# Fetching more of a graph layer's edge tiles by rows, and a later fall of GpSimd's lead

## The chip, the cores and the metric

The kernel runs on one core of one Trainium2 chip. A core has five engines that run their own instruction streams and wait for each other through semaphores: TensorE (PE in the profile, its weight loads PEld), VectorE (DVE), ScalarE (ACT), GpSimd (POOL) and SyncE (SP). Transfers are started by instructions on SP, ACT or POOL and are carried out by the core's 16 DMA engines. The metric is the device time of one execution in microseconds (us), lower is better.

## The reference, cut to what matters

A relational graph layer with 12500 nodes, 256 features, 8 relations and 212500 edges; the edges are sorted by their destination, and each node has an edge to itself.

```python
h = relu(layernorm(x))                       # 12500 x 256
hx = einsum('ni,rio->rno', h, weight)        # 8 relations
msg = hx[edge_type, src]                     # one row for each edge
agg = segment_sum(msg, dst, 12500)
out = x + agg * sqrt(0.5) + bias + (h @ loop_weight) * sqrt(0.5)
```

## The kernel before, in words

The sum over the edges is taken before the product with the weights: for each relation and destination node the rows of h of the edges' sources are added up, and the result is multiplied by the weight of that relation.

**Tiles.** The edges are cut into tiles of 128, two tiles to a unit. For a tile the 128 source rows of h (1 KB each) are brought from the chip's memory into a buffer `msg`, one row to a partition. VectorE makes a one-hot matrix `oh` of the edges' destinations and relations (L1066). TensorE multiplies the two (`edge_sums`, L1105: four matmuls in the profile for a tile, 6296 in all, so 1574 tiles), VectorE adds a unit's sums into a ring `acc` of node columns (L1141). When a group of 128 nodes is complete, 18 products with `w` and `wl` (L1321, two matmuls each in the profile) are spread between the next tiles' sums, VectorE adds the result to x (L1307, L1338), and SyncE stores it.

**How a tile's rows arrive.** There are two ways. Most tiles are gathered by GpSimd with one indirect DMA (L1009, `gather`). Some tiles are fetched by rows (`single_rows`, `begin_fetch`, `load_sources`): SyncE and ScalarE load the 128 source offsets into registers (L1030, five loads: two on SP for 28 and 32 rows, three on ACT for 24, 20 and 24 rows) and issue a DMA of 1 KB for every row (L1038), 60 on SP and 68 on ACT. GpSimd does nothing for such a tile. Before, the tiles with t % 54 of 25 or 53 are fetched in this way from tile 161 on, and besides them the last tile and the fifteenth from the end: 54 tiles. The first tiles, gathered from x and normalised by ScalarE in place, are all GpSimd's.

**The order of the work** is written out by hand: one loop over the tiles `t` emits the instructions of all engines, and each engine executes its own in that order. At tile t the loop emits the gathers up to `goal(t)`: the lead of GpSimd over the sums is 64 tiles at first, falls to 24 (`NEXT`), and near the end by one for every `SLOPE` = 5 tiles down to 8 (`CLOSE`). A gather also waits for the last finished unit of sums at that place, so the lead is a limit at run time too. A fetch by rows is begun 40 tiles ahead of its use (`FAR`), its instructions stand from 8 tiles later (`HOLD`) at up to four on each of the two engines for each tile. The buffers are a pool of 33 pairs, given out in the order of the loop; the first row or gather into a buffer waits for the sums that read it last. TensorE waits for all 128 rows of a fetched tile through a counter (L1101).

After the first 190 us or so ScalarE has hardly anything but the rows to do: its queue holds them and five small loads (`spans`, L441) that a later block of edges needs on VectorE. SyncE's queue also has the loads of x and h for the groups (`xr`, `hr`, L1258), the edges' indices (L432) and the stores of the results (L1350).

Of the kernel before, what the change touches and what calls it, by code (L numbers as in the profile page):

```python
# [40 lines left out]
NEAR = 8  # L41
# [17 lines left out]
SLOPE = 5  # L59
NEXT = 24  # L60
CLOSE = 8

SINGLE = 54
PLACED = (25, 53)
CLOSING = 15
SOONER = 64
FETCH = 4
SOURCES = ((0, 28, "SP"), (28, 24, "ACT"), (52, 20, "ACT"), (72, 32, "SP"), (104, 24, "ACT"))
# [193 lines left out]
def kernel(  # L262
# [22 lines left out]
    NT = plan.NT  # L285
# [57 lines left out]
    with ExitStack() as main:  # L343
# [623 lines left out]

        def in_turn(t):

            return t % SINGLE in PLACED  # L970

        def filled(t):

# [2 lines left out]

        def single_rows(t):

            return ((t in (NT - 1, NT - CLOSING) or in_turn(t) and t + 2 * NEAR < NT)
                    and state["h32"] is not None and t // QUAD * QUAD >= state["h32"] + LATE + AHEAD)  # L980

        def begin_fetch(t):
# [10 lines left out]
        def gather(t):  # L993
            if t % PAIR == 0 and t not in msg:
                room(t)
            if t % QUAD:
                kind[t] = kind[t - 1]
            else:
                kind[t] = "h" if state["h32"] is not None and t >= state["h32"] + LATE else "x"
            table = {"h": h32, "x": x}[kind[t]]  # L1000
            b, i, u = place_of(t)
            if single_rows(t) and t not in fetched and t - done["tile"] >= FAR:
                begin_fetch(t)
            if t in fetched:
                return
            at = i * P + u
            n = filled(t)
            of = direct[:, i : i + 1] if t < PAIR else gidx[b][:, at : at + 1]
            i = nc.gpsimd.indirect_dma_start(  # L1009
                out=msg[t][:n], out_offset=None, in_=table[:, :],  # L1010
                in_offset=bass.IndirectOffsetOnAxis(ap=of[:n], axis=0))
            if kind[t] == "h":
                n = landed[t] = len(landed)
                i.then_inc(landings[n % LANDINGS], 16)
                tc.no_tile_sem_insts.add(i.ins.name)
                tc.add_to_no_dep_group(f"landed{t}", i.ins)
            if "unit" in latest:
                tc.add_manual_dep(
                    i.ins, latest["unit"], SYNC_DEP, reason="no faster than the sums")

        def goal(t):

            lead = max(NEXT, AHEAD - max(0, t - NARROW) // SLOPE)
            lead = min(lead, max(CLOSE, (NT - t) // SLOPE))
            return min(t + lead + 1, STARTED + STEEP * (t // PAIR * PAIR))

        def load_sources(t, r0, count, engine):
# [364 lines left out]
        with tc.manual_schedule():  # L1392
# [150 lines left out]
            for t in range(NT):  # L1543
                done["tile"] = t
                if t + FAR >= gathered and single_rows(t + FAR):
                    begin_fetch(t + FAR)
                while gathered < min(NT, goal(t)):
                    gather(gathered)
                    gathered += 1
# [125 lines left out]
```

## Time and profile before

| What | Value |
| --- | --- |
| Time of the kernel before, median of 3 runs | 1936.13 us (1932.9 to 1936.15) |
| The profiled execution's own time | 1932.58 us |
| Its span from the first to the last instruction | 1930.9 us |
| Busy share of the span: PE, DVE, POOL, ACT | 87%, 69%, 75%, 7% |
| Mean granted TensorE clock | 0.96 |
| Gathers of h by GpSimd | 1432 |
| Rows fetched on ACT and on SP | 3672 and 3240 |

A line of a group has the line of the kernel, the engine, the operation, what it writes and reads, the count, then busy time and the mean in ns of one, then the engine's idle time just before and what ended it. In the lists of one source line, "min/median/max" are durations in ns, and the two times behind them are the starts of the first and the last instruction in us from the span's start. Instructions that issue DMAs or load registers on SP and ACT (SPq, ACTq) are not counted as busy: ACT's 7% says nothing of how full its queue is.

### The profile page before, as it was taken

The numbers are of one execution on the slowest core, as the hardware profiler recorded it, in microseconds if no ns is written. First come the engines' busy times: TensorE is split into PE (matmuls) and PEld (weight loads), VectorE is DVE, ScalarE is ACT, GpSimd is POOL, SyncE is SP. The second block draws the span as 40 slices with busy tenths as digits, with TensorE's granted clock in tenths as the row PEclk, the third lists the DMA queues.
The fourth block names the chain that finished last, engine by engine and source line by source line (L and its number), as shares of the span: only waits on it lengthen the run. The fifth ranks groups of instructions, "written<-read, shape, count | busy, mean of one in ns | idle before, by whom it ended". The sixth has DMA issues, their size and how long they took to land.

```text
span 1930.9 us, 41561 instructions
## 1 busy us (share of the span) xinstructions
PE 1684.4 (87%) x10136; PEld 1441.3 (75%) x10136; DVE 1325.9 (69%) x3353; ACT 132.0 (7%) x286; POOL 1445.7 (75%) x1546
## 2 busy tenths in 40 slices
PE   2367999999889999989888989898989888999998
PEld 2356889899778777777777777777777777777887
DVE  7888768976567965658766656776566885665653
ACT  6964000000000000000000000000000000000000
POOL 7777777777777777777777777777777777777774
PEclk9568999999999999999999999999999999999999
DMA  9974455445544444454444454444445444444443
GB/s 322 382 222 146 121 141 142 142 132 141 145 126 140 123 131 138 126 144 130 132 131 121 136 139 131 130 130 132 131 128 142 122 130 132 132 127 132 128 109 88
DMA packets 159057, 278.88 MB, mean 144 GB/s; under 512 B 35819, under 2 KB 110168, under 8 KB 158808
## 3 DMA queue, kind: packets, MB, share of 16 engines
q0 software_dynamic: 72960, 199.33, 36.3%
q1 hardware_dynamic: 77000, 73.08, 12.3%
q10 hardware_dynamic: 8848, 3.78, 1.0%
q8 instruction: 80, 1.31, 0.3%
q14 instruction: 169, 1.38, 0.2%
HBM read 250.45 MB, written 25.60 MB: 143 GB/s over the span
## 4 chain that ended last, share of the span: by engine, by line
PE 31%; POOL 27%; DMA 20%; issue 11%; DVE 7%; ACT 3%; DVEq 0%; SPq 0%; POOLq 0%; ACTq 0%
POOL msg L1009 27%; DMA msg<-h,gidx 19%; PE po L1321 16%; PE ps L1105 15%; ACT msg L931 1%; DVE acc L1141 1%; DVE stats L887 1%; DMA xt<-in_x_dram 1%; DVE oh L1066 1%; DVE moves L478 1%; ACT xt L931 1%; DVE acc L1183 1%; PE pt L1165 1%; ACT acc L1154 0%; DVE fixed L480 0%
## 5 line engine op out<-in xcount | busy, mean ns | idle before, releaser
L1009 POOL DMA_INDIRECT msg<-h,gidx x1432 | 1360.2, 950 | 439.1 <-issue 375.9
L1105 PEld LDWEIGHTS ps<-oh,msg 128*128 128x128 f32 x6296 | 915.7, 196 | 384.7 <-DMA msg<-h,gidx 261.9
L1105 PE MATMUL ps<-oh,msg 128*128 128x136 f32 (+1 forms) x6296 | 998.9, 288 | 197.6 <-DMA msg<-h,gidx 131.5
L1321 PE MATMUL po<-w,acc 128*128 128x256 f32 (+1 forms) x3136 | 881.5, 386 | 4.2 <-DVE acc L1141 3.0
L1141 DVE TENSOR_TENSOR acc<-acc,ps 128x352 f32 x788 | 406.5, 516 | 363.0 <-PE ps L1105 351.3
L1321 PEld LDWEIGHTS po<-w,acc 128*128 128x128 f32 (+1 forms) x3136 | 515.3, 192 | 42.0 <-issue 11.3
L1183 DVE SCALAR_TENSOR_TENSOR acc<-types,pt 128x256 f32<-128x256 bf16 x720 | 258.9, 412 | 76.0 <-PE pt L1165 65.3
L1066 DVE TENSOR_TENSOR oh<-fixed,cols 128x544 f32<-128x544 f32 x394 | 281.4, 714 | 0.0
L1321 PE MATMUL po<-wl,self_t 128*128 128x256 f32 (+1 forms) x392 | 111.8, 409 | 5.4 <-DVE self_t L1170 4.6
L1009 POOL DMA_INDIRECT msg<-in_x_dram,gidx x86 | 81.5, 948 | 26.2 <-issue 23.5
L1321 PEld LDWEIGHTS po<-wl,self_t 128*128 128x128 f32 (+1 forms) x392 | 71.2, 203 | 13.5 <-DVE self_t L1170 5.9
L1307 DVE TENSOR_TENSOR xr<-xr,po 128x256 f32<-128x256 f32 (+1 forms) x98 | 40.5, 413 | 19.1 <-PE po L1321 19.0
L1338 DVE TENSOR_TENSOR xr<-xr,po 128x256 f32<-128x256 f32 (+1 forms) x98 | 41.2, 421 | 10.4 <-PE po L1321 7.0
L478 DVE TENSOR_SCALAR moves<-fixed 128x336 int32<-128x336 int32 (+1 forms) x96 | 44.6, 465 | 5.2 <-DVE acc L1141 3.7
L931 ACT ACTIVATE msg<-msg,shift,rstd 128x256 f32<-128x256 f32 x88 | 44.8, 587 | 6.9 <-DVE stats L895 4.5
L480 DVE COPY_PREDICATED fixed<-moves,fixed 128x335 int32<-128x335 int32 (+7 forms) x96 | 41.6, 433 | 3.3
L1237 DVE CAST types<-pt 128x512 bf16<-128x512 f32 x23 | 15.9, 690 | 40.0 <-PE pt L1233 39.1
L1170 DVE COPY self_t<-pt 128x256 f32<-128x256 f32 (+1 forms) x98 | 40.6, 414 | 2.2 <-PE pt L1165 2.2
L1165 PE MATMUL pt<-ident,hr 128*128 128x128 f32 (+1 forms) x196 | 38.3, 278 | 2.9 <-DMA hr<-h 1.5
L931 ACT ACTIVATE xt<-xt,shift,rstd 128x256 f32<-128x256 f32 x66 | 33.7, 587 | 9.8 <-DVE shift L928 9.8
L1221 DVE TENSOR_TENSOR of<-pt,line 22x512 bf16<-22x512 f32 x23 | 15.7, 682 | 20.4 <-PE pt L1214 20.2
L1165 PEld LDWEIGHTS pt<-ident,hr 128*128 128x128 f32 (+1 forms) x196 | 25.3, 149 | 5.3 <-DMA hr<-h 1.8
(179 smaller groups left out, 373.8 us busy)
## 6 DMA issues: line engine op xcount, KB each, us to landing
msg<-h ACTq DMA_DIRECT2D x3672, 1.0 KB
msg<-h SPq DMA_DIRECT2D x3240, 1.0 KB
msg<-h,gidx POOLq DMA_INDIRECT x1432, 5.1
hr<-h SPq DMA_DIRECT2D x23, 512.0 KB
xr<-in_x_dram SPq DMA_DIRECT2D x23, 512.0 KB
out_dram<-xr SPq DMA_DIRECT2D x22, 512.0 KB
xt<-in_x_dram SPq DMA_DIRECT2D x16, 512.0 KB
h<-xt SPq DMA_DIRECT2D x16, 512.0 KB
```

What stands on the lines that cost most here:

```text
L478: nc.vector.tensor_single_scalar(m, packed[:, :n], 1 << (bit + k), op=ALU.bitwise_and)
L480: nc.vector.copy_predicated(packed[:, : n - (1 << k)], m[:, 1 << k :], packed[:, 1 << k : n])
L931: nc.scalar.activation(row, row, AF.Relu, bias=shift[:n, j : j + 1], scale=rstd[:n, j : j + 1])
L1009: i = nc.gpsimd.indirect_dma_start(out=msg[t][:n], out_offset=None, in_=table[:, :], in_offset=bass.IndirectOffsetOnAxis(ap=of[:n], axis=0))
L1066: j = nc.vector.tensor_tensor(o[:, k : k + v, :i, :width], iota_f[:, :width].unsqueeze(1).unsqueeze(1).to_broadcast([P, v, i, width]), of. ...
L1105: j = nc.tensor.matmul(ps[:, c, first : first + width], m[:used, c * P : (c + 1) * P], o[:used, :width], start=(i == 0 and c == 0), stop=( ...
L1141: i = nc.vector.tensor_tensor(a, a, ps[:, c], op=ALU.add)
L1165: in_run("turns", nc.tensor.transpose(pst[:, c, :n], rows_[:n, c * P : (c + 1) * P], ident[:n, :n]), c == KC - 1)
L1170: nc.vector.tensor_copy(got["self", g][:, :, :n], pst[:, :, :n])
L1183: i = nc.vector.scalar_tensor_tensor(acc[:, :, r, s0 : s0 + n], of, float(r + 1), pst[:, :, :n], op0=ALU.is_equal, op1=ALU.mult)
L1321: i = nc.tensor.matmul(got["out", g][:n], lhs, rhs, start=(r == R and c == 0), stop=(r == R - 1 and c == KC - 1))
L1338: nc.vector.tensor_add(rows_[:n, k, :], rows_[:n, k, :], got["out", g][:n])
```

## The change: what it does

```diff
-SINGLE = 54
-PLACED = (25, 53)
-CLOSING = 15
+SINGLE = 24
+PLACED = 13
+ENDING = 2
...
         def in_turn(t):
 
-            return t % SINGLE in PLACED
+            return t % SINGLE == PLACED
...
         def single_rows(t):
 
-            return ((t in (NT - 1, NT - CLOSING) or in_turn(t) and t + 2 * NEAR < NT)
+            return ((t == NT - 1 or in_turn(t) and t + 2 * NEAR < NT)
                     and state["h32"] is not None and t // QUAD * QUAD >= state["h32"] + LATE + AHEAD)
...
         def goal(t):
 
             lead = max(NEXT, AHEAD - max(0, t - NARROW) // SLOPE)
-            lead = min(lead, max(CLOSE, (NT - t) // SLOPE))
+            lead = min(lead, max(CLOSE, (NT - t) // ENDING))
             return min(t + lead + 1, STARTED + STEEP * (t // PAIR * PAIR))
```

A tile is now fetched by rows when t % 24 is 13, from tile 157 to tile 1549, and the last tile, 1573, which is again 24 tiles on. That is 60 tiles instead of 54, with a distance of 24 instead of 28 and 26 in turn. The fifteenth tile from the end is gathered. The division of a fetched tile between SP (60) and ACT (68) stays. The lead of the gathers falls from 24 when 48 tiles are left (before: 120) and reaches 8 at 16 (before: 40).

On GpSimd six gathers fewer stand in the queue; these are its rows of gathers (`direct` and `x` are the first tiles, `flag` is read at the end):

```order
 L1009 DMA msg<-in_x_dram,direct 128x256 x2
 L1009 DMA msg<-in_x_dram,gidx 128x256 x86
-L1009 DMA msg<-h_57,gidx 128x256 x1432
+L1009 DMA msg<-h_57,gidx 128x256 x1426
 L1638 TENSOR_LOAD flag
 L1648 COMPARE_AND_BRANCH
```

Six gathers left, and nothing else of GpSimd's moved.

On ScalarE this is the place of the first `spans` load among the rows of the first fetched tiles (`single` holds the offsets of the sources):

```order
 L1030 TENSOR_LOAD single
 L1038 DMA msg<-h_57 1x1024 x24
+L1030 TENSOR_LOAD single
+L1038 DMA msg<-h_57 1x1024 x24
+L1030 TENSOR_LOAD single
+L1038 DMA msg<-h_57 1x1024 x20
+L1030 TENSOR_LOAD single
+L1038 DMA msg<-h_57 1x1024
 L441 DMA spans<-in_dst_dram 128x2x1
```

45 rows and three loads of registers more stand ahead of the `spans` load here; between a fetched tile's rows and the next one's there is no other instruction on this engine, before and now.

On SyncE this is the place where the first fetched tile begins; `hr` is a load of four groups' rows of h. Before:

```order
L1258 DMA xr<-in_x_dram 128x4x256
L1258 DMA hr<-h_57 128x4x256 x2
L1030 TENSOR_LOAD single
L1038 DMA msg<-h_57 1x1024 x28
L1030 TENSOR_LOAD single
```

And now:

```order
L1258 DMA xr<-in_x_dram 128x4x256
L1258 DMA hr<-h_57 128x4x256
L1030 TENSOR_LOAD single
L1038 DMA msg<-h_57 1x1024 x11
L1258 DMA hr<-h_57 128x4x256
L1038 DMA msg<-h_57 1x1024 x17
```

One load of `hr` now stands behind the first rows of the first fetched tile. TensorE's and VectorE's instructions stand in the same order as before.

## The prediction

> **What bounds the kernel now.** I read the page's sums and chain first, then GpSimd by stretches and row by row, then the two queues that fetch rows, because the change moves tiles from the one to the others.
>
> ```profile
> span 1930.9 us, 41561 instructions
> PE 1684.4 (87%) x10136; PEld 1441.3 (75%) x10136; DVE 1325.9 (69%) x3353; ACT 132.0 (7%) x286; POOL 1445.7 (75%) x1546
> ...
> PE 31%; POOL 27%; DMA 20%; issue 11%; DVE 7%; ACT 3%; DVEq 0%; SPq 0%; POOLq 0%; ACTq 0%
> ```
>
> PE has the larger busy share, but the chain runs through POOL, its issue gaps and the landing of its gathers for more than half of the span. Gathers by stretches (POOL busy), four of POOL's rows near the end, and its waits after 1780 us:
>
> ```profile
> 200.00:300.00 100.00, 75.78 (x80) 1.00 0.49 135
> 900.00:1000.00 100.00, 75.59 (x81) 0.97 0.47 132
> 1800.00:1900.00 100.00, 75.60 (x81) 0.98 0.42 117
> ```
> ```profile
> 1779.53 0.95 POOL L1009 DMA_INDIRECT msg<-h,gidx  x1 [0.30 <-issue]
> 1780.78 0.95 POOL L1009 DMA_INDIRECT msg<-h,gidx  x1 [0.30 <-issue]
> ...
> 1910.85 0.95 POOL L1009 DMA_INDIRECT msg<-h,gidx  x1 [0.30 <-issue]
> 1912.10 0.95 POOL L1009 DMA_INDIRECT msg<-h,gidx  x1 [0.30 <-issue]
> ```
> ```profile
> POOL msg L1009 <- issue: 25.9, 85, 0.3
> POOL msg L1009 <- PE ps L1105: 6.7, 22, 0.3
> ```
>
> The pace never changes: 107 gathers start between 1779.53 and 1912.10, so one every 132.57/106 = 1.2507 us, and 0.3 us is the longest gap, whatever ended it. GpSimd works without a pause; its "75%" is 0.95 of 1.25 us. It is the bound, with TensorE just behind:
>
> ```profile
> PEld ps L1105 <- DMA msg<-h,gidx: 261.9, 401, 3.0
> ```
>
> TensorE waits for gathers 401 times. It has the room to run faster:
>
> ```profile
> 900.00:1000.00 100.00, 89.46 (x526) 74.38 (x524) 76.10 (x198) 0.00 (x0) 75.59 (x81) 0.97 0.47 132
> ```
>
> **The rows' own queues.** ScalarE's 7% hides its queue. Rows and register loads over the run, and SP's waits:
>
> ```profile
> L1038 ACTq DMA_DIRECT2D msg<-h x3672: 227/228/804, 198.4 to 1865.8; - x194
> L1038 SPq DMA_DIRECT2D msg<-h x3240: 224/228/1812, 198.4 to 1858.9; - x191
> ```
> ```profile
> L1030 ACTq TENSOR_LOAD <-single x162: 1532/1790/2890, 182.4 to 1855.9; - x162
> ```
> ```profile
> SPq L1038 <- PE ps L1105: 304.6, 43, 47.5
> ```
>
> 54 tiles of 68 rows; at present the queues wait for free buffers (SP 43 times), so rows come well before their use. What a fetched tile costs ACT when nothing holds it is read from three places: the rows alone of one tile, the loads of three tiles near the end, and the loads of fourteen tiles early on.
>
> ```profile
> L1038 ACTq DMA_DIRECT2D msg<-h x23: 227/228/233, 666.1 to 673.3; - x23
> ```
> ```profile
> L1038 ACTq DMA_DIRECT2D msg<-h x68: 227/228/470, 1202.0 to 1227.9; - x68
> L1038 SPq DMA_DIRECT2D msg<-h x60: 227/228/304, 1202.0 to 1224.3; - x60
> ```
> ```profile
> L1030 ACTq TENSOR_LOAD <-single x7: 1582/1819/1832, 1780.4 to 1837.9; - x7
> ```
> ```profile
> L1030 ACTq TENSOR_LOAD <-single x43: 1539/1783/1903, 224.5 to 635.1; - x43
> ```
>
> A row takes 7.2/22 = 0.33 us of the queue (0.23 is the DMA, the rest a register move and gaps). One tile: 25.9 us from its first row to its last, two loads among them, 0.2 for the last row, 1.8 for the load ahead and 0.2 of gaps, 28.1 us. Near the end (57.5 us for two tiles) 28.75; with the third, of 28.1, 28.5 on average. Early on 410.6/14 = 29.3 us a tile, row behind row. SP's 60 rows need 22.5 and two loads of about 2.1, one of them inside: 25 us.
>
> **The change, part by part.**
>
> GpSimd: six gathers fewer, 6 x 1.2507 = 7.5 us. If it stays the bound, the last gather ends 7.5 us earlier and 1932.58 becomes 1925.1. TensorE could follow: 24 tiles cost it 24 x 1.2 x 0.89 = 25.7 us of work, by the stretch 900 to 1000 (83 tiles, 89% busy), where GpSimd gives it 24 tiles in 23 x 1.2507 = 28.8.
>
> ScalarE: 28.8 us is also all that it now has for a fetched tile, where it had 26 x 1.2507 = 32.5 on average. Its own need was 28.1 to 29.3. So the question of this change is whether one queue keeps up, and it is settled by a sum over the run: 60 tiles, one after the other, in one stream.
>
> It can't start sooner than the buffer is free. The first row was held until 198.4 us by the sums of the tile 66 before; the first fetched tile is now 157 instead of 161, and tiles go by at one a microsecond there:
>
> ```profile
> 200.00:300.00 100.00, 57.45 (x396) 57.36 (x395) 1.00 0.49 135
> 300.00:400.00 100.00, 57.86 (x400) 57.74 (x398) 1.00 0.50 142
> ```
>
> 396/4 = 99 tiles in 100 us, so it starts 4 us sooner, at 194.4, and its rows are out 26.1 us later (as before, where the second tile's first load is at 224.5), at 220.5. 59 tiles follow, then the last rows land, and behind them come the last tile's sums and the tail. This is the tail, with the last products:
>
> ```profile
> 1914.97 2.56 PE ps L1105 x20
> ...
> 1917.95 7.19 PE po L1321 x32
> ```
>
> The last tile's four matmuls start 0.7 us before 1917.53, at 1916.8, so the tail is 1930.9 - 1916.8 = 14.1 us. For the landing no view gives the rows alone; the gathers on the same chip, with rows running all the time (300 to 500 us) and with pauses (900 to 1100 us), took
>
> ```profile
> DMA to landing us min/median/max: 7.1/11.4/12.2
> ```
> ```profile
> DMA to landing us min/median/max: 3.3/4.6/5.9
> ```
>
> from the issue on. I take 6 us, between 4 and 11. With c us for a tile and the 1.7 us around the span: 1.7 + 220.5 + 59c + 6 + 14.1 = 242.3 + 59c. Before's 1932.58 is reached at c = 28.65, GpSimd's 1925.1 at 28.5.
>
> Which c? Bounds are 28.1 and 29.3. The early row is the state to which the change leads: SP and ACT without a pause, and gathers landing late. From tile 157 TensorE passes 24 tiles in 24 us while ACT needs 29, so the 40 us by which the rows are ahead (tile 157's sums are due 66 tiles after tile 91's, at about 261) are used up after eight tiles, near tile 350. From there on TensorE waits at every fetched tile; SP, which needs less, comes to be held by buffers, which eases the traffic a little. I take 29.3 for the first 15 of the 59 and 28.8 for the other 44, above the 28.5 of the end, because that stretch began after pauses: 439.5 + 1267.2 = 1706.7, so 242.3 + 1706.7 = **1949.0 us**, 16 us over the profiled execution.
>
> TensorE's waits for rows do not add to this: the work of 24 tiles fits into c, and GpSimd's gathers run ahead meanwhile, up to 24 tiles, which is one whole distance.
>
> The lead at the end I cost at nothing: GpSimd never waited more than an issue gap after 1780 us, so a limit that it doesn't reach may be eased for free. If TensorE stands at tile 1549 for its rows, the old rule would have allowed 8 tiles ahead, leaving 16 gathers, 20 us, still inside the 28.8 before the last tile's rows; without that cover it would be worth up to 16 gathers' part beyond it, none here. The gather in place of the fifteenth tile's rows is in the six.
>
> What stands behind the rows: on SP one `hr` load moves behind rows that wait until 194, its users come 30 us and more later; on ACT the `spans` loads of 0.4 us, which VectorE needs some 30 us after their present issue:
>
> ```profile
> 281.82 0.41 ACTq L441 DMA_DIRECT2D spans<-in_dst_dram  x1
> ```
>
> With ACT late that cover shrinks to about ten tiles, 10 us. Nothing; if it is gone, a few us at each of five places, in which TensorE mostly waits anyway.
>
> Two rules of the Trainium skill speak against my sum; both lead to the first rival below. The Trainium skill's page "DMA: Bandwidth & Descriptors", section "Latency and other measured facts", has a floor of about 0.6 us for a register load; by it the three would take 1.8 us, c would be 25 and the answer 1925. The rows above show 1.79 for each one, and they decide. The same page of the Trainium skill, section "Issuing engines are not separate DMA queues", says that all queues share the 16 engines and that several issuers save only issue time, usually small beside the transfer; by it the rows would cost no queue anything and the answer would again be 1925. The later landing fits its first half; its second doesn't fit the 28 us of issue for a tile.
>
> **The rivals.**
>
> *GpSimd stays the bound* (the other side: faster). It needs c up to 28.6 over the whole run. For it: single tiles of 28.1, and the last three. Against it: fourteen in a row of 29.3, without a pause as now. Price: 1925.1 up to c = 28.5, then rising to 1932.
>
> *A tie.* c between 28.64 and 28.78 gives 1932 to 1940; ScalarE takes away what GpSimd gains. For it: the 28.75 of the two tiles from 1780 on.
>
> *The traffic feeds on itself.* Rows never pause, landings stay at 11 us, and c stays at 29.3 to the end: 242.3 + 5 + 59 x 29.3 = 1976. Against it: the transfers for groups and indices are spread over a longer time, and SP will pause.
>
> *The change doesn't do what it says*: the end's lead is such a part; it moves no time in any of the cases.
>
> **How the numbers follow.** Forecast (c from 28.78 to 29.2) 0.56; GpSimd stays the bound 0.18; tie 0.13; traffic 0.13. What can be told from no change is 0.2%, some 4 us around 1936.13, so from 1932.3 to 1940: faster 0.18, same 0.13, slower 0.69. The time is the forecast's, 1949. It is made against 1932.58, and the median shown is 3.6 above that; I don't add this, because what sets the time changes. The forecast's own range is 1940 to 1965. Taking in GpSimd's 1925.1 and most of the traffic's case leaves about 0.15 outside: 1925 to 1970.
>
> **What would show it.** Right: ACT's loads at three per 28.8 us or more from the first to the last, without a wait for buffers after the first tile; its last row near 1925; TensorE's largest waits now for the rows (L1105 or its counter at L1101, on `msg<-h` from ACT) from about 450 us on, and fewer for gathers; GpSimd with pauses longer than 0.3 us behind the sums, and fewer than 80 gathers in 100 us. Wrong: GpSimd still at 1.25 us without a pause, its last gather near 1904.6, and ACT waiting for buffers. Also wrong in size: c well under 28.6 because rows come faster when GpSimd is slowed, or a tail longer than 14 us.

## The result, and the profile after

The change makes the kernel slower: 1965.36 us median of four runs (1961.28 to 1966.87) against 1934.68 us for the kernel before (1932.9 to 1936.15), a ratio of 1.016 with a 95% interval of 1.0146 to 1.0174. The forecast was 1949.0 us. The profiled execution took 1961.28 us, 28.7 us more than the profiled one of before; the forecast had 16.4 us. The median lies 16.4 us above the forecast: 12.3 of them are in the profiled execution, and the other 4.1 are there because the profiled execution was the quickest of the four. The direction and the mechanism were right, the size was not.

The chain of waits of the kernel after, first by engine, then by line:

```profile
ACTq 43%; PE 27%; DMA 10%; issue 10%; DVE 4%; ACT 4%; SPq 2%; PEldq 0%; DVEq 0%
ACTq L1038 35%; PE po L1321 14%; PE ps L1105 12%; DMA msg<-h 9%; ACTq L1030 8%; ACT msg L931 2%; SPq L1038 1%; DVE stats L887 1%; ACT xt L931 1%; DVE acc L1141 1%; ACT acc L1154 0%; DMA nat_s<-in_src_dram 0%; PE pt L1214 0%; DVE oh L1066 0%; ACT unused L900 0%
```

Before, ScalarE's queue had 0% of this chain and POOL 27%. Now ScalarE's row issues (L1038) and register loads (L1030) have 43%, the landing of the rows 9%, and POOL is gone from it. The list of waits says the same from the other side (columns: total us, times, longest):

```profile
PEld ps L1105 <- PEq L1101: 197.7, 47, 9.9
PE ps L1105 <- PEq L1101: 181.2, 47, 9.5
POOL msg L1009 <- PE ps L1105: 82.4, 157, 3.6
```

L1101 is the counter of a fetched tile's rows. TensorE waits there at 47 of the 60 fetched tiles, and its 261.9 us of waits for gathers are no longer in the list. GpSimd, which before stood still for 0.3 us at most once 200 us were over, now waits up to 3.6 us for sums, because its lead is used up. By stretches (the fifth pair of columns is POOL):

```profile
200.00:300.00 100.00, 96.14 (x637) 88.42 (x636) 71.26 (x163) 0.00 (x0) 75.59 (x81) 1.00 0.49 136
400.00:500.00 100.00, 83.16 (x509) 74.47 (x507) 58.08 (x132) 0.00 (x0) 69.53 (x73) 0.91 0.46 125
1200.00:1300.00 100.00, 84.47 (x521) 77.19 (x522) 73.15 (x177) 0.00 (x0) 75.54 (x80) 0.93 0.47 126
```

TensorE is busy 96% until the head start of the rows is spent, and GpSimd loses gathers (73 in place of 80) where its lead first runs into the limit. The rows and the register loads on the queues:

```profile
L1038 ACTq DMA_DIRECT2D msg<-h x4080: 227/228/552, 195.7 to 1942.1; - x195
L1038 SPq DMA_DIRECT2D msg<-h x3600: 224/228/2792, 195.7 to 1887.3; - x190
...
L1030 ACTq TENSOR_LOAD <-single x180: 1446/1787/2987, 183.1 to 1932.7; - x180
```

From the end of each tile's last row on ScalarE (records of L1038, 68 to a tile) the first tile was out at 221.8 us, the sixteenth at 667.4 and the sixtieth at 1942.4. So a fetched tile took (1942.4 - 221.8)/59 = 29.16 us of ScalarE's queue: 445.6/15 = 29.7 in the first fifteen, 1275.0/44 = 28.98 in the others. The last tile's sums:

```profile
1943.59 2.71 PE L1105 MATMUL ps<-oh,msg 128*128 128x104 f32 x20
1946.74 7.17 PE L1321 MATMUL po<-w,acc 128*128 128x256 f32 x32 [0.43 <-DVE acc L1141]
```

The four matmuls of the last tile start some 0.7 us before 1946.3, so 1945.5; the landing was 3.1 us and the tail 1959.6 - 1945.5 = 14.1. The prediction's sum with measured terms is 1.7 + 221.8 + 59 x 29.16 + 3.1 + 14.1 = 1961.1, and the execution took 1961.28.

### The profile page after: what moved, and what is told of

It reads as the page before. It is cut to its first block, busy times and chain, and to the rows that moved or that the text cites. A ratio compares the mean times of both kernels' runs of the same rounds, so it can differ in the third digit from the quotient of the medians.

```text
span 1959.6 us, 43202 instructions
## 1 busy us (share of the span) xinstructions
PE 1662.4 (85%) x10136; PEld 1504.6 (77%) x10136; DVE 1323.5 (68%) x3353; ACT 132.0 (7%) x286; POOL 1440.4 (74%) x1540
## 3 DMA queue, kind: packets, MB, share of 16 engines
q14 instruction: 182, 1.49, 0.3%
## 4 chain that ended last, share of the span: by engine, by line
ACTq 43%; PE 27%; DMA 10%; issue 10%; DVE 4%; ACT 4%; SPq 2%; PEldq 0%; DVEq 0%
ACTq L1038 35%; PE po L1321 14%; PE ps L1105 12%; DMA msg<-h 9%; ACTq L1030 8%; ACT msg L931 2%; SPq L1038 1%; DVE stats L887 1%; ACT xt L931 1%; DVE acc L1141 1%; ACT acc L1154 0%; DMA nat_s<-in_src_dram 0%; PE pt L1214 0%; DVE oh L1066 0%; ACT unused L900 0%
## 5 line engine op out<-in xcount | busy, mean ns | idle before, releaser
L1105 PEld LDWEIGHTS ps<-oh,msg 128*128 128x128 f32 x6296 | 960.9, 202 | 339.3 <-PEq L1101 197.7
L1105 PE MATMUL ps<-oh,msg 128*128 128x136 f32 (+1 forms) x6296 | 976.0, 288 | 244.2 <-PEq L1101 181.2
L1321 PE MATMUL po<-w,acc 128*128 128x256 f32 (+1 forms) x3136 | 914.5, 398 | 6.0 <-DVE acc L1141 4.5
L1321 PEld LDWEIGHTS po<-w,acc 128*128 128x128 f32 (+1 forms) x3136 | 534.4, 199 | 49.1 <-issue 11.7
L1237 DVE CAST types<-pt 128x512 bf16<-128x512 f32 x23 | 15.9, 690 | 37.9 <-PE pt L1233 37.4
L1221 DVE TENSOR_TENSOR of<-pt,line 22x512 bf16<-22x512 f32 x23 | 15.7, 682 | 27.4 <-PE pt L1214 27.3
```

Of the source, the lines that this page charges most:

```text
L1105: j = nc.tensor.matmul(ps[:, c, first : first + width], m[:used, c * P : (c + 1) * P], o[:used, :width], start=(i == 0 and c == 0), stop=( ...
L1321: i = nc.tensor.matmul(got["out", g][:n], lhs, rhs, start=(r == R and c == 0), stop=(r == R - 1 and c == KC - 1))
```

## The experiments

There were eighteen runs. The first fourteen fell on chips on which before itself takes 2389 to 2418 us in place of 1935, so every ratio here is to runs of before on the same chip.

### On the chips of 1935 us

**Rows 72 to 103 by one transfer (less_rows_e).** ScalarE issues what the change issues; SyncE issues 28 single rows and one transfer of 32 rows in place of 60 single ones, and has one register load in place of two. TensorE's counter waits for 97 arrivals in place of 128.

```diff
+            if r0 == 72:
+                def fetch_block(k=fetched[t]):
+                    j = nc.sync.dma_start(msg[t][r0 : r0 + count, :], h32[:count])
...
-                j = nc.tensor.wait_ge(counters[k % COUNTERS], 16 * P * (k // COUNTERS + 1))
+                j = nc.tensor.wait_ge(counters[k % COUNTERS], 16 * (P - 31) * (k // COUNTERS + 1))
```

> The change with rows 72 to 103 of every fetched tile fetched by one transfer of 32 neighbouring rows of h; those are not the rows of the sources, so this part of the result is not the reference's. Where before takes about 1935 us: on ScalarE's records of the change a row takes 337 ns while SyncE issues none and 347 ns while it does, 0.7 us a tile, and sp52_less gained 1.5 us a tile from 27 rows fewer; by that ScalarE's tile falls from 29.16 to 28.2 to 28.6, 1925 to 1930 us, ratio 0.995 to 0.998. If the surplus is ScalarE's own: 1.011 to 1.016. Where before takes about 2400 us: 0.986 again.

Measured: 1927.54 us against 1934.72, ratio 0.9964 (0.995 to 0.9978), as the theory of the traffic has it; 1927.54 is 7.2 us below before, and six gathers are 7.5. Its chain, its waits and ScalarE's rows (line numbers are 13 higher):

```profile
ACTq 38%; PE 27%; issue 11%; POOL 8%; DMA 7%; DVE 5%; ACT 3%; SPq 0%; DVEq 0%; PEldq 0%; POOLq 0%
```
```profile
POOL msg L1009 <- issue: 401.3, 1315, 0.3
...
PEld ps L1118 <- PEq L1114: 115.4, 40, 5.9
PEld ps L1118 <- DMA msg<-h,gidx: 79.7, 131, 2.2
...
POOL msg L1009 <- PE ps L1118: 44.4, 140, 2.0
```
```profile
L1051 ACTq DMA_DIRECT2D msg<-h x4080: 227/228/858, 194.5 to 1902.6; - x195
```

The same 4080 rows are issued 39.5 us sooner. Reckoned as above, a tile takes 28.51 us of ScalarE's queue in place of 29.16. From the records the 68 issues of a tile last 16.58 us together in place of 17.17, and of them 3.8 in place of 7.4 last over 300 ns; the three loads (5.2 and 5.3 us) and the rest, register moves and gaps (6.7 in both), are what they were. No gap on ScalarE is over 1 us in either run behind the first fetched tile, so its queue is not held by buffers. So 0.59 of the 0.65 us is row issues that had been drawn out beside SyncE's single rows. 28.51 is just under GpSimd's 23 x 1.2507 = 28.77: both queues are about equal, waits for gathers are back, and GpSimd keeps its pace.

The traffic shows in the gathers too. The last column is the median time from issue to landing in us; the view has a landing for 21 of the gathers before, for 126 in less_rows_e and for 21 in even64_e. Before:

```profile
msg<-h,gidx POOLq DMA_INDIRECT x1432, 5.1
```

with the transfer of 32 rows:

```profile
msg<-h,gidx POOLq DMA_INDIRECT x1426, 2.8
```

and with 64 single rows on each engine (the next run):

```profile
msg<-h,gidx POOLq DMA_INDIRECT x1426, 9.5
```

The landings of more gathers can be read from the semaphores' updates: a gather's landing is told by sixteen increments, and over a thousand gathers of each run have all sixteen. The fifteenth comes 2.8 us after the issue (median) in all four kernels, the sixteenth after 5.1 us before, 9.3 in the change, 3.2 in less_rows_e and 9.5 in even64_e. So one of the sixteen is late, and the more so the more single rows there are. The single rows themselves stand in line: each is one packet of 1 KB that lasts 0.06 to 0.09 us, but a ScalarE row's packet, taken in the order of issue, ends 2.8 us after its issue before (median), 7.0 in the change, 1.3 in less_rows_e and 9.1 in even64_e. This would fit single rows that all go through one of the 16 DMA engines; the trace doesn't number the engines, so that place is argued, not shown.

The Trainium skill's page "DMA: Bandwidth & Descriptors", section "Issuing engines are not separate DMA queues", says that transfers of all issuers interleave on the same 16 engines; these landings agree. Its remark that the issue is usually small beside the transfer does not hold for rows of 1 KB: here the issue sets the time, and 32 issues on one queue lengthen those of the other.

**64 rows on each engine (even64_e).**

```diff
-SOURCES = ((0, 28, "SP"), (28, 24, "ACT"), (52, 20, "ACT"), (72, 32, "SP"), (104, 24, "ACT"))
+SOURCES = ((0, 32, "SP"), (32, 24, "ACT"), (56, 16, "ACT"), (72, 32, "SP"), (104, 24, "ACT"))
```

> The change split 64 to 64. Where before takes about 1935 us: ScalarE's tile is 27.8 us, under GpSimd's 28.8, so GpSimd is the bound again: 1925 to 1928 us, ratio 0.995 to 0.997; if the loss is not ScalarE's queue, 1.016. Where before takes about 2400 us: 1.073 again.

Measured: 1947.08 us against 1934.72, ratio 1.0062 (1.0048 to 1.0077). The split is worth some 18 us against the change (1.0062 for 1.016), so the rival that it is worth nothing falls; but the kernel is still slower than before, so the expectation falls too. Chain, waits, and the rows:

```profile
SPq 35%; PE 28%; DMA 15%; DVE 9%; issue 9%; ACT 3%; DVEq 0%; PEldq 0%; ACTq 0%
```
```profile
PEld ps L1105 <- PEq L1101: 192.9, 41, 13.4
```
```profile
L1038 SPq DMA_DIRECT2D msg<-h x3840: 227/228/1729, 193.6 to 1919.6; - x192
L1038 ACTq DMA_DIRECT2D msg<-h x3840: 227/228/776, 193.6 to 1880.9; - x192
```

ScalarE is done 61 us sooner than in the change and has 0% of the chain; SyncE has taken its place. From the first tile's end (217.5 us) to the last's (1919.9) a tile took SyncE 28.85 us on average, not 26.4. One tile in this mean took 46.2 us: SyncE stood still ahead of two loads of the edges' indices, which the profile puts down to the landing of earlier loads:

```profile
SPq L432 <- DMA hr<-h: 9.9, 1, 9.9
SPq L436 <- DMA nat_s<-in_src_dram: 6.5, 1, 6.5
```

The 44 tiles ahead of this stop took 28.87 us each without a gap of 1 us, which is already over GpSimd's 28.77; the 14 behind it took 27.56. What the kernel would take without the stop no run shows. The last rows needed 10.7 us to land: 1.7 + 217.5 + 59 x 28.85 + 10.7 + 14.1 = 1946.2, where the profiled execution took 1946.59. I had costed SyncE's tile from 25 us, one tile's rows and two loads. In the change's own trace its first eighteen tiles, with next to no pauses, took 26.3, 26.7 and 27.4 us (means of six), with 0.5 to 1.1 us for the loads of x and h that go through the same queue, and row issues that grew as on ScalarE. The four rows brought their own cost and again longer issues: 64 of them last 16.57 us, 259 ns each, where the change's 60 last 14.55, 242 ns each.

**The fetched tiles of before, split otherwise (b56, b52).** The kernel before with its 54 fetched tiles, and 56 to 72 and 52 to 76 rows.

```diff
-SOURCES = ((0, 28, "SP"), (28, 24, "ACT"), (52, 20, "ACT"), (72, 32, "SP"), (104, 24, "ACT"))
+SOURCES = ((0, 24, "SP"), (24, 24, "ACT"), (48, 24, "ACT"), (72, 32, "SP"), (104, 24, "ACT"))
```

For b52 the last four ranges are (24, 24) and (48, 28) on ScalarE, (76, 28) on SyncE and (104, 24) on ScalarE.

> The kernel before (54 fetched tiles, its places and its lead at the end) with four rows of a fetched tile moved from SyncE to ScalarE: 56 to 72. Where before takes about 2400 us: SyncE's tile falls from about 37.5 to 36.8 us when nothing holds it, ScalarE's rises to 35 to 36.5, both under the 40.2 us that 26.2 tiles take there; if SyncE's queue bounds the second half of before, as its head start of 1 us at the end says, the time falls to the 0.985 to 0.995 that fewer rows on SyncE gave at best (less_rows); if not, 1.00. Where before takes about 1935 us: ScalarE's tile is 30.5 us against 32.5 between fetched tiles, so no change, 0.999 to 1.002.

> The kernel before with eight rows moved: 52 to 76. Where before takes about 2400 us: SyncE 36.1 us, ScalarE 37.3 (measured in sp52_b), still under 40.2: as b56, 0.985 to 0.995 if SyncE's queue bounds before, 1.00 if not. Where before takes about 1935 us: ScalarE's tile is 31.8 us against 32.5, no room left: 1.000 to 1.005.

Measured: 1935.62 and 1936.93 us against 1936.08, ratios 0.9995 (0.9981 to 1.001) and 1.0003 (0.9988 to 1.0018). ScalarE's tile took 31.68 us in b52 (31.8 expected) and still fits into the 32.5 between fetched tiles of before. So 76 rows on ScalarE cost nothing while the distance is longer, and the change's 68 cost some 30 us when it is shorter: it is the distance against the queue that counts. ScalarE has no gap over 1 us in b52, so the 31.68 us are its own.

### On the chips of 2400 us

There instructions of SyncE and ScalarE come at longer intervals. In rows_alone, from the records, the mean step from one row to the next, with no load between, is 0.55 us on SyncE and 0.42 on ScalarE, where the change has 0.34 and 0.35; the durations of the issues (239 to 252 ns on average in before and the change on the chips of 1935 us, 206 and 243 here) are not what grew. SyncE is the longer queue.

**The rows alone, the lead alone, every 26th tile (rows_alone, end_alone, every26, every26_b).** The first is the change with before's lead at the end, the second before with the change's lead at the end, the third the change with `SINGLE = 26`.

```diff
-            lead = min(lead, max(CLOSE, (NT - t) // ENDING))
+            lead = min(lead, max(CLOSE, (NT - t) // SLOPE))
```

> The changed kernel with the old fall of the lead at the end (from 120 tiles left). Theory: ScalarE's stream is the same, 1961 to 1967 us. Rival C: most of the loss is gone, 1926 to 1935 us.

> The kernel before with the lead's fall at the end alone changed: it stays at 24 until 48 tiles are left. Theory: GpSimd never reaches this limit, so nothing: 1932 to 1937 us, ratio 0.999 to 1.001. Rival C (the lead at the end does harm, because gathers then crowd the last rows' transfers): slower by 5 us or more.

> The changed kernel with every 26th tile fetched by rows instead of every 24th, split 60 and 68 as before. Theory (ScalarE's stream): the distance is now 25 gathers, 31.3 us, more than ScalarE's 29.2, so ScalarE keeps up and GpSimd is the bound: before's 1933 less 1.25 us for each fetched tile above 54, so 1930 to 1932 us, and no waits for rows. Rival A (traffic of rows, as a steep load): between before and the changed kernel, 1940 to 1950 us.

> The change with every 26th tile fetched in place of every 24th, split 60 to 68 as in the change (55 fetched tiles, 1431 gathers: one fewer than before). The distance is now 25 gathers of 1.2507 us = 31.3 us for a fetched tile, over the 29.2 of ScalarE's queue. The theory: GpSimd is the bound, ratio 0.998 to 1.001. The rival (regular spacing or the traffic of rows costs by itself): ratio 1.01 or more. Where before takes about 2418 us: as in the first four experiments, about 1.013, with SyncE's queue as the longer one.

Measured: the rows alone 1.0387 (1.0333 to 1.044), the lead alone 1.0009 (0.9989 to 1.003, ten runs), every 26th tile 1.0127 (1.0085 to 1.0168) and again 1.0093 (1.0063 to 1.0123). The lead is worth nothing, as it was costed, and the loss is in the rows. Every 26th tile costs something on these chips; on those of 1935 us it was not tried. The chain of waits with the rows alone:

```profile
SPq 47%; issue 31%; PE 12%; DVE 5%; another core or an unknown queue 2%; DMA 1%; ACT 1%; DVEq 0%; PEldq 0%; ACTq 0%
```

And of the kernel with before's rows and the new lead, which is as fast as before:

```profile
SPq 33%; issue 28%; PE 27%; DVE 9%; another core or an unknown queue 2%; ACT 1%; DMA 0%; DVEq 0%; ACTq 0%; PEldq 0%
```

SyncE's queue has a third of the chain there already, and its last rows come 1 us ahead of their use, where the first came 67 us ahead.

**64 to 64 (even64, even64_b, even64_c, even64_d).** The edit is that of even64_e.

> The changed kernel, with SyncE fetching 64 rows of a fetched tile and ScalarE 64 (instead of 60 and 68); everything else as changed. Theory (ScalarE's stream of rows and register loads is the bound: 60 tiles in series at 29.2 us each, measured in the changed kernel's profile): four rows fewer at 0.33 us make 27.8 us a tile, under the 28.8 that GpSimd's 23 gathers take, so GpSimd is the bound again: about 1925 us, ratio to before 0.995 to 0.997, no pauses on GpSimd after 200 us, no waits for rows at L1101. Rival A (the DMA traffic of 128 rows in so short a distance is the bound, whoever issues them): nothing changes, 1961 to 1966 us. Rival B (TensorE's lower granted clock, 0.92, is the cause): 1961 to 1966 us too, with the clock still at 0.92 while TensorE is busy without waits.

> The change with its rows split 64 to 64 (four rows of every fetched tile go from ScalarE to SyncE), once more, beside its own runs of before. The theory: the bound after the change is the queue that issues the fetched rows, whichever is longer per tile, and else GpSimd at 1.25 us a gather. Where before takes about 1935 us (SyncE's row as quick as ScalarE's): ScalarE's time per tile falls from 29.16 us by 4 rows of 0.33 us to 27.8, SyncE's rises from 25 to 26.4, both below 23 x 1.2507 = 28.8, so GpSimd is the bound again and the time is 6 gathers below before, 1925 to 1928 us, ratio 0.995 to 0.997. Where before takes about 2418 us (the first four experiments): SyncE's queue was the longer there, so the ratio is again 1.07. A rival: the loss of the change does not come from the row queue but from the traffic of the single rows as a whole or from TensorE's lower granted clock; then the split is worth nothing and the ratio stays near 1.016.

> The change with its rows split 64 to 64, on a third chip. What the two queues take for a tile decides, and before's own time on the chip tells which case it is. Where before takes about 1935 us: ScalarE's 27.8 us and SyncE's 26.4 are both under GpSimd's 28.8, so 1925 to 1928 us, ratio 0.995 to 0.997; the rival (the loss does not come from ScalarE's queue) gives 1.016 as the change. Where before takes about 2400 us: 1.073 for the third time, SyncE's queue being the longer there.

> The change split 64 to 64. Where before takes about 1935 us: GpSimd is the bound again, 1925 to 1928 us, ratio 0.995 to 0.997; if the loss is not ScalarE's queue, 1.016. Where before takes about 2400 us: 1.073, with SyncE's queue the longer.

Measured: 1.0728, 1.0728, 1.0737 and 1.0735, intervals no wider than 1.0675 to 1.0785. The first expectation, made for a chip of 1935 us, failed; the others knew the chip. Four rows more on SyncE nearly double the loss of the rows alone, with TensorE and GpSimd as they were.

**52 to 76, and with fewer rows beside it (sp52, sp52_b, sp52_less).** sp52 is the change with b52's split, sp52_less the same with SyncE's rows 76 to 103 by one transfer, as in less_rows_e.

> The change with eight rows of every fetched tile moved the other way, from SyncE to ScalarE: 52 to 76. The theory, that the time goes with the longer of the two row queues, wants opposite signs on the two kinds of chip. Where before takes about 1935 us: ScalarE's tile grows from 29.16 us by 8 rows of 0.33 us to 31.8, so 240.6 + 59 x 31.8 = 2117 us, ratio 1.09. Where before takes about 2400 us (SyncE's row takes 0.54 us there, ScalarE's 0.42): SyncE's tile falls from 37.5 us by 8 x 0.54 to 33.2, ScalarE's rises from 33 to 36; the longer is 36 in place of 37.5, so 59 x 1.5 = 88 us less than the 2513.7 of the change without the new lead, ratio 1.00 to 1.02 where that was 1.039. The rival, that the loss comes from single rows as such or from TensorE's clock, has no change of ratio with the split on either.

> The change split 52 to 76 once more, as the reference for sp52_less on the same chip. Where before takes about 2400 us: ratio 1.036 again, ScalarE's queue the bound at 37.2 us a tile. Where before takes about 1935 us: 31.8 us a tile, about 2117 us, ratio 1.09.

> sp52 with SyncE's 28 rows 76 to 103 of a tile fetched by one transfer of 28 neighbouring rows of h; those are not the rows of the sources, so this part of the result is not the reference's. ScalarE's queue issues the same 76 rows and three loads and is the bound in both. If SyncE's single rows lengthen ScalarE's (the rival of the prediction, in a weak form), ScalarE's tile falls by 0.5 us or more and the time by 30 us or more against sp52_b. If the length of a row issue is ScalarE's own, the time is within 15 us of sp52_b.

Measured: sp52 1.0364 (1.033 to 1.0397), not 1.00 to 1.02; sp52_b 1.0418 (1.0374 to 1.0461); sp52_less 1.0019 (0.9995 to 1.0043), 94 us below sp52_b. Chain and rows of sp52_b:

```profile
ACTq 49%; issue 21%; PE 16%; DVE 8%; another core or an unknown queue 4%; DMA 1%; ACT 1%; DVEq 0%; SPq 0%; PEldq 0%
```
```profile
L1038 ACTq DMA_DIRECT2D msg<-h x4560: 3/228/877, 247.7 to 2487.0; - x199
L1038 SPq DMA_DIRECT2D msg<-h x3120: 3/227/1487, 247.7 to 2414.1; - x195
```

Rows of sp52_less:

```profile
L1051 ACTq DMA_DIRECT2D msg<-h x4560: 2/228/825, 244.2 to 2394.2; - x199
```

The bound went over from SyncE to ScalarE (SPq from 47% to 0%, ACTq from 0% to 49%) and found no shorter queue there: 37.4 us a tile on ScalarE (37.2 in sp52), where SyncE had 37.5. My 36 for it was too low. With 27 issues fewer on SyncE the same 76 rows take ScalarE 35.8 us a tile, 1.54 less, 59 x 1.54 = 91 of the 94 us. Here most of it, 1.49 us, is time between ScalarE's row issues and loads (register moves and gaps), not the length of the issues as on the chips of 1935 us. Nor do the rows stand in line here: a ScalarE row's packet ends 1.1 us after its issue (median) in both kernels. So the two kinds of chip don't show the same cause, and why the gaps shrink here is open.

**less_rows and less_rows_c** are less_rows_e on these chips.

> The change, but SyncE's rows 72 to 103 of every fetched tile come by one transfer of 32 neighbouring rows of h in place of 32 single ones; those are not the rows of the sources, so this part of the result is not the reference's. ScalarE's queue issues what it did (68 rows, three loads). It tells apart where the 29.16 us of a tile on ScalarE come from beyond the 28.1 that a tile took with pauses. If it is single-row traffic that shares the DMA engines with ScalarE's (the rival that the traffic feeds on itself): ScalarE's tile falls to 28.1 to 28.5, GpSimd is nearly the bound, 1925 to 1930 us, ratio 0.995 to 0.998. If it is ScalarE's own (the time that its rows and loads take behind each other): it stays at 29.0 to 29.2, about 1955 to 1961 us, ratio 1.011 to 1.016. Where before takes about 2418 us and SyncE's queue is the bound: SyncE loses nearly half of its rows, and the time falls to before's or below, ratio 0.99 to 1.00, without telling the two apart.

> As less_rows: the change, but rows 72 to 103 of every fetched tile come by one transfer of 32 neighbouring rows of h, which are not the rows of the sources, so that part of the result is not the reference's. Where before takes about 1935 us: if single-row traffic beside ScalarE's lengthens its tile, it falls to 28.1 to 28.5 us and the time to 1925 to 1930 us (ratio 0.995 to 0.998); if the surplus over 28.1 us is ScalarE's own, 1955 to 1961 us (1.011 to 1.016). Where before takes about 2400 us: 0.985 again.

Measured: 0.9853 (0.9816 to 0.989) and 0.9875 (0.9843 to 0.9907). PE has 66% of the chain in less_rows_c and the queues have none: where SyncE is relieved, the kernel is faster than before there.

**two_23** (even64 with two loads on ScalarE and every 23rd tile) doesn't compute the reference's result. By the kernel's text, every second one of its fetched tiles has an even number, and `single` holds the source offsets of the odd tiles alone (L469, L1031), so these tiles get the rows of their neighbour. The amount of work is that of the right rows. Its ratio was 1.0842 (1.0785 to 1.09), with SyncE's queue again the longer.

> A version meant to beat both: 64 rows on each engine, ScalarE's with two register loads in place of three, and every 23rd tile fetched (1424 gathers, eight fewer than before). ScalarE's time per tile: 64 rows of 0.33 us and two loads of about 2.1 us, 25.3 us, with the surplus of about 1 us that the change showed 26.3; SyncE's the same; GpSimd's distance is 22 x 1.2507 = 27.5 us. Theory: GpSimd is the bound, eight gathers below before: 1923 to 1926 us, ratio 0.994. Rival: the queues' time per tile grows with the closer spacing beyond 27.5 us and the time is over before's, ratio 1.00 to 1.02. Where before takes about 2418 us: SyncE's queue is the bound, ratio 1.08 or more.

No version with all rows of the reference beat before.

## Why the prediction was right or wrong, point by point

- **GpSimd bounds before, one queue of rows bounds after**: right. The chain went from POOL to ACTq, and the sum over one stream of 60 tiles gives the profiled time to 0.2 us once its terms are measured. Moving four rows to SyncE (even64_e) took the end from ScalarE to SyncE; on the chips of 2400 us sp52 did the reverse.
- **The failed step: "I take 29.3 for the first 15 of the 59 and 28.8 for the other 44".** The mechanism held, and this term of its sum was too small. It was 29.7 and 28.98, on average 29.16 in place of 28.93. The sum's term 1706.7 was 1720.5: 13.8 us too little, because 59 tiles multiply an error of 0.23 us. Of the other terms the first tile's end came 1.3 us late (221.8 for 220.5) and the landing took 3.1 us in place of 6; 13.8 + 1.3 - 2.9 = 12.2 is the whole of the 12.3 us between 1949.0 and 1961.28. The landing's error of 2.9 us the other way was luck: the views it was taken from hold three gathers each. The 3.6 us by which the median of before lay above its profiled execution were not added, "because what sets the time changes"; after the change the median lay 4.1 us above its own profiled execution, so that reason did not hold.
- **Why c was low**: the first five tiles took 29.3 us, as the early stretch of before did, but the next ten took 29.7 and 30.1 (means of five), the state that the fourteen tiles of before had not reached; and the 28.8 came from two tiles behind a pause, where the queues now hardly pause. What lengthens a tile is the other queue's rows: less_rows_e takes 0.65 us off by thinning SyncE's rows, with every row and load of ScalarE's kept. I named this traffic, but gave it too little weight once SyncE is held by buffers: its pauses are only 3 to 4.6 us of a tile (means of six, from tile nineteen on).
- **Rival "the traffic feeds on itself" (29.3 to the end, 1976)**: half right. The traffic lasts, but at 28.98, and the landing at the end was 3.1 us, not 11. Its landing did appear in even64_e, 10.7 us, where both queues ran nearly without a pause (16.4 us in two gaps on SyncE, 10 us in three on ScalarE).
- **Rival "GpSimd stays the bound" (1925)**: false for the change, true for less_rows_e (1927.5), where c is 28.51: the switching point of 28.5 to 28.65 was right.
- **The head start**: forecast to be used up after eight tiles, near tile 350 and 450 us. ScalarE's last row came 41 us ahead of its use at the first tile and 11 at the seventh, tile 301; since the rows still have to land, TensorE waits from about 400 us on.
- **Signs**: three loads and no wait for buffers on ScalarE, waits at L1101, pauses of GpSimd, all as forecast. Its last row was to come near 1925 and came at 1942. Fewer than 80 gathers in 100 us were seen only between 400 and 800 us: later 23 gathers (28.77 us) nearly fill a tile of 28.98.
- **The end's lead at nothing**: right as far as tried (end_alone, 1.0009, on the chips of 2400 us); on those of 1935 us it was not tried alone.
- **SyncE "needs less, 25 us"**: too low by 1.3 to 2.4 us for the queue without a pause. It did not matter for the change and did for even64_e.

## What to carry to other kernels

A queue that only issues small transfers can be the bound while its engine shows 7% busy: add up its issues, register loads and other transfers for one period and compare with the period of the engine it relieves. When two such periods are within a few per cent, take the cost from a stretch in which both queues run without pause, since an error of 0.23 us was multiplied by 59, and count how far each queue lengthens the other. Before moving work from the longer queue to the shorter, cost the shorter one with everything that already goes through it.

## What the runs showed of the hardware that was not expected

- Single rows of 1 KB from two queues slow each other: 32 row issues fewer on SyncE took 0.65 us off a ScalarE tile of 29.16 (27 issues fewer took 1.54 off 37.4 on the slower chips, there in the gaps). Where both queues ran with next to no pause, they issued the same number of rows per us together: 4.5 in the first eighteen tiles of the change (68 rows in 29.7 us and 60 in 26.8) and 4.5 in even64_e ahead of its stop (64 in 28.0 and 64 in 28.9). That looks like a limit of its own, and the rows standing in line for 7 to 9 us in both speak for it; two splits are few, so it is not shown.
- The gathers' landing follows the single rows, by one of its sixteen increments: that one comes after a median of 3.2, 5.1, 9.3 and 9.5 us in less_rows_e, before, the change and even64_e, the fifteenth after 2.8 us in all.
- The granted TensorE clock was lower where TensorE waited for rows: 0.921 on average after against 0.960 before, 0.922 in even64_e and 0.936 in less_rows_e. The sum over ScalarE's queue gives the change's time without the clock; what lowers it is open.
- One kernel differs by a quarter between chips (1935 and 2389 to 2418 us), and with it the bound: GpSimd on the one, SyncE's row queue on the other. What lengthens the steps between instructions there is open.
